# Moving a small partial result to another buffer and reordering VectorE's work in a fused cross-attention kernel

## The chip, the cores and the metric

The kernel runs on one core of a Trainium2 chip. The metric is the device time of one execution in microseconds (us). Engines are named as in the profile: PE is TensorE's matmul stream and PEld its weight loads, DVE is VectorE, ACT is ScalarE, POOL is GpSimd, SP is SyncE, which here only issues transfers. A queue named SPq or POOLq is the stream of transfers that this engine issues.

## The reference

For each of 8 batches, with x1 and x2 of shape 512 x 1024 (channels by positions), Wq and Wk of 64 x 512 and Wv of 512 x 512, all in fp32:

```python
q = jnp.einsum('bcn,dc->bnd', x1, Wq) + bq
k = jnp.einsum('bcn,dc->bdn', x2, Wk) + bk[:, None]
v = jnp.einsum('bcn,dc->bdn', x2, Wv) + bv[:, None]
attn = jax.nn.softmax(jnp.einsum('bnd,bdm->bnm', q, k), axis=2)
attn_out = jnp.einsum('bcm,bnm->bcn', v, attn)
return attn_out + x1
```

## The kernel before, in words

**What is multiplied.** The value projection and the attention product are taken in another order: first y = x2 times the exponentials of the scores (512 channels by 1024 query positions), then out = Wv times y, plus bias, plus x1. Both of these are done by Strassen's scheme (Winograd's form) over 2 x 2 blocks: seven block products instead of eight, at the price of sums of blocks on DVE, on transfers that add, and in PSUM. For y the seven products carry the numbers 1, 2, 6, 7, 5, 3, 4, and most of these are themselves done by the same scheme one level down. The function `multiply_seeded` does one such product: seven inner products named by steps 1, 7, 6, 2, 5, 4, 3 in this order. It needs left sums (`left_stream`, line 569, four DVE instructions) and right sums (`right_stream`, lines 599, 604 and 606, three DVE instructions) ahead of it.

**What one product does on ACT.** Inside `multiply_seeded`, PE accumulates steps 1, 6, 5 and 4 in one PSUM tile, the chain, and ACT copies the chain after each of them into the quarters of the product's two result banks b0 and b1 (line 858). Step 7 goes to a second PSUM tile, the third. ACT copies it to SBUF as a small tile v, also at line 858. Only after these copies can PE go on adding into the chain. At the end DVE adds v into bank b1; this is `complete`, line 875. In the profile the chain of product 5 is ps_i5chain, its third ps_i5third, its banks ps_ya, and the v of every product is just v.

**How work is ordered.** The order on each engine is the order in which the program is written; there is no scheduler. `period(s, n, nn, nnn)` is one batch: s is the batch whose y and output are made, n the next one, whose scores and exponentials are made at the same time, nn and nnn the ones after. Batches are counted from 0. `s.six` is true for batches 2 to 5, in which product 6 of y is also done by the inner scheme and products 6 and 7 are joined. For such a batch the stretch that matters runs on PE as follows: scores of batch n, queries of nn (ps_q, line 192), product 7, product 5, product 3, more scores of n (ps_s, line 237), and then the keys of nn (ps_k, line 192).

**Buffers and waits.** An SBUF tile is asked for with a tag. Two tiles with the same tag and one buffer share the same memory, so the first write to the later tile waits for everything that still reads or writes the earlier one, transfers too. Four tags count here:

- `r` holds, within one batch, v of product 5, v of product 3, v of product 4, and then the output block 12 of the batch (uo3 in the program). That block gets x1 added by a POOL transfer and is stored by an SP transfer (lines 1058 and 1059, `out_dram<-uo` in the profile), both issued in the next batch.
- `yT4` holds the left sums of product 7 and later the sum T4 of y.
- `a12` holds a block of x2, and then the left sums of product 3.
- `eT2` holds T2, a sum of exponential blocks that two POOL transfers read (line 386, `eT<-eT`), and then the right sums of product 3.

**The row sums.** `shares` inverts the softmax's row sums of one half: a DVE reciprocal (line 320), a POOL transfer to memory (line 321), and a POOL transfer that spreads them over the partitions (line 327, `den<-row`). `lower` subtracts the maximum from the next batch's scores (DVE, line 342). `copy_7` copies product 7's two banks to SBUF, negated (ACT, line 975); its second call reads bank b1, so it comes after product 7's `complete`. `join_67` adds that to product 6 (DVE, line 970).

**The lines that the change touches** are those between product 7 and product 5 of `period`. Product 7's matmuls are recorded earlier; `complete_7` is its joining on DVE.

Of the kernel before, what the change touches and what calls it, by code (L numbers as in the profile page):

```python
# [15 lines left out]
def kernel(  # L16
# [295 lines left out]
    def invert(s, h):  # L312

        few = s.few[h]
        s.row[h] = row = dram.tile([1, H], F32, tag="row", name=f"row_{s.b}_{h}")
        to = row.rearrange("o (p f) -> (o p) f", p=P)
        if h == 0 and s.b > 1:
            nc.vector.tensor_tensor(few[:, 0, :], few[:, 0, :], few[:, 1, :], ALU.add)
            to = row.rearrange("o (z p f) -> (o p) z f", z=2, p=D)
        nc.vector.reciprocal(few, few)  # L320
        nc.gpsimd.dma_start(to, few)

    def spread(s, h):

        s.rden[h] = s.den[h]
        queue = nc.sync if s.b >= B - 2 else nc.gpsimd
        queue.dma_start(s.rden[h], s.row[h].broadcast_to([P, H]))

    def shares(s, h):
        invert(s, h)  # L330
        spread(s, h)
# [7 lines left out]
    def lower(s, h, i):  # L339
        e = s.e[h][:, :, i, :]  # L340
        top = s.top[h].unsqueeze(1).to_broadcast([P, 2, H])
        nc.vector.tensor_tensor(e, e, top, ALU.subtract)  # L342
# [193 lines left out]
    def weave(*streams):  # L536

        streams = list(streams)
        while streams:
            for stream in list(streams):  # L540
                if next(stream, "end") == "end":
                    streams.remove(stream)
# [19 lines left out]
    def left_stream(s, i, x, tag):  # L562

        v = {f"{p + 1}{q + 1}": x[:, ts(q, MH // 2), ts(p, P)] for p in range(2) for q in range(2)}
        sums = sb.tile([P, 4, MH // 2, P], F32, tag=tag, name=f"aI{i}_{s.b}")
        s.inner[i] = v
        for z, (k, x, y, op) in enumerate(LEFT_SUM if i in (1, 2) else LEFT):
            v[k] = sums[:, z]
            nc.vector.tensor_tensor(v[k], v[x], v[y], op)  # L569
            yield  # L570
# [4 lines left out]
    def right_stream(s, i, x, *tags):  # L575

        half = x.shape[1] // 2
        v = {f"{q + 1}{r + 1}": x[:, ts(q, half), ts(r, H // 2)] for q in range(2) for r in range(2)}
        last = 4 // len(tags)
        shape = [P, last, half, H // 2]  # L580
        sums = [
            sb.tile(shape, F32, tag=t, name=f"eI{i}{t}_{s.b}") if isinstance(t, str) else t for t in tags
        ]
        if i in (1, 2):
            for z, k in enumerate(("T1", "T2", "T4", "T3")):
                v[k] = sums[z // last][:, z % last]
            s.inner[i, "t"], s.inner[i, "m"] = v, sums[-1][:, last - 2 : last]
            for k, x, y, op in (
                ("T3", "22", "12", ALU.add),
                ("T2", "T3", "11", ALU.subtract),  # L590
                ("T1", "12", "11", ALU.subtract),
                ("T4", "21", "T2", ALU.subtract),
            ):
                nc.vector.tensor_tensor(v[k], v[x], v[y], op)
                yield
            return
        both, t2, t4 = sums[0][:, 0:2], sums[-1][:, last - 2], sums[-1][:, last - 1]
        part = x.rearrange("p (q k) (r n) -> p q k r n", q=2, r=2)
        nc.vector.tensor_tensor(
            both, part[:, :, :, 1, :], part[:, 0].rearrange("p k r n -> p r k n"), ALU.subtract  # L600
        )
        s.inner[i, "t"] = v | {"T1": both[:, 0], "T3": both[:, 1], "T2": t2, "T4": t4}
        yield
        nc.vector.tensor_tensor(t2, both[:, 0], v["22"], ALU.subtract)
        yield
        nc.vector.tensor_tensor(t4, v["21"], t2, ALU.add)
        yield

    def inner_right(s, i, x, *tags):
        weave(right_stream(s, i, x, *tags))  # L610

    def inner_product(s, i, z, ps, opens, *copies):

        ka, kb, _, _ = MULT[z]
        n_k = s.inner[i][ka].shape[1]
        for k in range(n_k):
            nc.tensor.matmul(  # L617
                ps,
                s.inner[i][ka][:, k, :],
                s.inner[i, "t"][kb][:, k, :],  # L620
                start=opens and k == 0,
                stop=z in (2, 3, 4) and k == n_k - 1,
                skip_group_check=True,
            )
        for copy in copies:
            nc.scalar.copy(copy, ps)

    def inner_parts(s, i):

        ks = ("third", "chain") if i in ((1, 6, 7) if s.six else (2, 7)) else ("chain", "third")  # L630
        of = {k: ps_s.tile([P, H], F32, tag="s", name=f"ps_i{i}{k}_{s.b}")[:, left] for k in ks}
        return of["chain"], of["third"]
# [202 lines left out]
    def multiply_seeded(s, i, v_tag, hooks={}, bank=None):  # L835

        bank = bank or MULT[i][2]

        def fresh(j):
            s.bank[bank, j] = ps = ps_a.tile(  # L840
                [P, H], F32, tag=f"{bank}{j}", name=f"ps_y{bank}{j}_{s.b}_{i}"
            )
            return ps

        b0 = fresh(0)
        chain, third = inner_parts(s, i)
        if v_tag == "top" or s.b == B - 1 and v_tag == "r":
            v = sb.tile([P, H], F32, tag="top", name=f"v{i}_{s.b}", bufs=2)[:, left]
        else:
            v = sb.tile([P, 2, H], F32, tag=v_tag, name=f"v{i}_{s.b}")[:, 0, left]  # L850
        seeded = s.six and i == 5
        if seeded:
            nc.scalar.copy(third, s.v6)

        def step(z, ps, opens, out=None, of=None):
            inner_product(s, i, z, ps, opens)
            if out is not None:
                nc.scalar.copy(out, of)  # L858
            if z in hooks:
                hooks[z]()  # L860

        step(1, chain, True, b0[:, left], chain)
        step(7, third, not seeded, v, third)
        if s.six and i == 6:
            s.v6 = v
        b1 = fresh(1)
        step(6, chain, False, b1[:, left], chain)
        step(2, b0[:, left], False)
        step(5, chain, False, b0[:, right], chain)
        step(4, b1[:, left], False, b1[:, right], chain)  # L870
        step(3, b0[:, right], False)

        def complete(b1=b1):
            b = b1.rearrange("p (a n) -> p a n", a=2)
            nc.vector.tensor_tensor(b, b, v.unsqueeze(1).to_broadcast([P, 2, H // 2]), ALU.add)

        return complete
# [91 lines left out]
    def join_67(s):  # L969
        nc.vector.tensor_tensor(s.tmp[6], s.tmp[6], s.tmp[7], ALU.add)  # L970

    def copy_7(s, j):
        if j == 0:
            s.tmp[7] = sb.tile([P, 2, H], F32, tag="u1", name=f"uy7_{s.b}")
        nc.scalar.mul(s.tmp[7][:, j, :], s.bank["c", j], -1.0)
# [253 lines left out]
    def period(s, n, nn, nnn):  # L1229
# [72 lines left out]
        if s.b == 0:  # L1302
# [30 lines left out]
            complete_5 = multiply_seeded(s, 5, "r")  # L1333
# [21 lines left out]
        else:  # L1355
# [78 lines left out]
            else:  # L1434
                complete_5 = multiply_seeded(s, 5, "top", {6: evict_q} if five and nn else {}, "a")
# [8 lines left out]
                    leave()  # L1444
            if n:
                sums_3 = right_stream(s, 3, s.t["22"], "eT2" if s.six else "eT1")
                next(sums_3)
                if s.b == 1:
                    shares(s, 1)
                weave(*([left_stream(s, 3, s.a["S4"], "a12" if s.six else "aI3")] if nn else []), sums_3)  # L1450
                if s.six:
                    complete_7()
                    shares(s, 1)
                lower(n, 0, 0)
            else:
                inner_right(s, 3, s.t["22"], "eT1")
            hooks = {}
            if s.six:
                lower(n, 0, 1)
                complete_5 = multiply_seeded(s, 5, "r", {7: lambda: copy_7(s, 0), 6: lambda: copy_7(s, 1)}, "a")  # L1460
                join_67(s)
                complete_5()
                evict_y(s, "22")
            else:
                complete_7 = multiply_seeded(s, 7, "y12")
                complete_7()
                hooks[7] = lambda: copy_7(s, 1)
                copy_7(s, 0)
# [237 lines left out]
    with tc.manual_schedule():  # L1706
        head(states[0])
        for b in range(B):
            period(*states[b : b + 4])
# [36 lines left out]
```

## Time and profile before

| what | value |
|---|---|
| median of 3 runs | 671.51 us (671.10 to 671.86) |
| the profiled execution's own time | 671.32 us |
| span of the profile, first to last instruction | 669.5 us |
| PE busy | 658.5 us, 98% |
| DVE busy | 619.1 us, 92% |
| ACT, POOL busy | 387.0 us (58%), 215.8 us (32%) |
| moved by transfers | 133.26 MB, mean 199 GB/s |
| granted TensorE clock | 1.000 |

The 1.8 us between the span and the execution's own time lie before the first and after the last instruction. The share of busy PE says that PE is nearly always occupied, so a change can gain only where PE stands still, or by giving PE less to do. The mean busy share of the core's 16 transfer engines appears as "DMA share"; it can come out a little over 1 in a short window.

### The profile page before, as it was taken

Reading aid. Unit: us, or ns where it says so; the run is one execution under the profiler, and the core shown is the slowest. Engines: PE = TensorE matmul, PEld = TensorE weight load, DVE = VectorE, ACT = ScalarE, POOL = GpSimd, SP = SyncE. Lnnn points to the kernel's source line nnn. Section 1 sums busy time; section 2 is a strip of 40 time slices with the busy share of each in tenths; the row PEclk is TensorE's granted clock in tenths of the full one; section 3 lists DMA queues with packets and bytes.
Section 4 is the critical chain, followed back from the end, with each engine's and each line's share of the span. In section 5 each row is a group of like instructions: output and inputs, shape, how many; then the busy total and the mean of one; then the engine's idle time right before and its main releaser. Section 6 shows DMA issues by size and latency. Waiting matters only on the chain.

```text
span 669.5 us, 8115 instructions
## 1 busy us (share of the span) xinstructions
PE 658.5 (98%) x2644; PEld 436.7 (65%) x2644; DVE 619.1 (92%) x900; ACT 387.0 (58%) x744; POOL 215.8 (32%) x187
## 2 busy tenths in 40 slices
PE   9999999999999999998999999999999999999997
PEld 4435755766668666776667676676765757657865
DVE  1999999989999899998989989999889999999996
ACT  3754457446485666764667646766467455484332
POOL 0126214621328203282033710346103640224300
PEclk9999999999999999999999999999999999999999
DMA  8688578994899959999599995989956895368614
GB/s 334 248 250 269 129 245 150 211 266 133 261 174 211 262 156 285 187 190 271 141 283 187 192 286 152 260 197 185 284 145 126 186 239 173 67 131 181 126 39 150
DMA packets 48522, 133.26 MB, mean 199 GB/s; under 512 B 5600, under 2 KB 6112, under 8 KB 48480
## 3 DMA queue, kind: packets, MB, share of 16 engines
q0 software_dynamic: 21488, 59.32, 48.7%
q1 hardware_dynamic: 26848, 73.29, 30.2%
q8 instruction: 21, 0.34, 0.2%
q10 hardware_dynamic: 144, 0.14, 0.1%
q14 instruction: 21, 0.17, 0.1%
HBM read 87.83 MB, written 16.81 MB: 156 GB/s over the span
## 4 chain that ended last, share of the span: by engine, by line
PE 83%; DMA 8%; DVE 5%; ACT 2%; issue 1%; SPq 0%; ACTq 0%
PE ps_yc L617 8%; PE ps_ya L617 7%; PE ps_oc L504 7%; DMA out_dram<-uo 6%; PE ps_s L237 5%; PE ps_ya L504 4%; PE ps_oa L504 4%; PE ps_k L192 3%; PE ps_oa L801 3%; PE ps_i4b L952 3%; PE ps_i3chain L617 3%; PE ps_i1chain L617 3%; PE ps_i2chain L617 3%; PE ps_i5chain L617 3%; PE ps_q L192 3%; PE ps_oc L952 2%
## 5 line engine op out<-in xcount | busy, mean ns | idle before, releaser
L342 DVE TENSOR_TENSOR e<-e,top 128x1024 f32<-128x1024 f32 x60 | 72.0, 1216 | 0.2 <-POOL top L274 0.2
L351 ACT ACTIVATE e<-e 128x1024 f32<-128x1024 f32 x60 | 62.9, 1060 | 15.8 <-DVE e L342 15.5
L274 POOL PARTITION_ALL_REDUCE top<-max x16 | 32.3, 2019 | 110.6 <-DVE max L268 51.7
L246 ACT COPY e<-ps_s 128x512 f32<-128x512 f32 x90 | 47.8, 623 | 9.7 <-PE ps_s L237 7.1
L237 PE MATMUL ps_s<-q,k 64*128 64x512 f32 (+1 forms) x188 | 46.6, 598 | 0.0
L306 POOL PARTITION_ALL_REDUCE den<-sum x10 | 33.3, 3333 | 31.4 <-DVE sum L268 26.5
L258 DVE TENSOR_TENSOR max<-max,e 128x1024 f32<-128x1024 f32 x30 | 36.5, 1218 | 0.3
L237 PEld LDWEIGHTS ps_s<-q,k 64*128 64x128 f32 x188 | 17.5, 186 | 19.9 <-issue 16.5
L987 DVE TENSOR_TENSOR y<-y,den 128x1024 f32<-128x1024 f32 x24 | 29.2, 1219 | 0.3
L858 ACT COPY ps_yc<-ps_i7chain 128x256 f32<-128x256 f32 x32 | 11.4, 357 | 28.9 <-PE ps_i7chain L617 15.1
L287 POOL PARTITION_ALL_REDUCE den<-sum x6 | 19.4, 3230 | 21.9 <-DVE sum L268 21.9
L192 PE MATMUL ps_q<-x_in_x_dram,wqk_sb 128*64 128x512 f32 x112 | 25.6, 598 | 0.4
L504 PE MATMUL ps_oc<-yT,w 128*128 128x512 f32 x56 | 25.3, 594 | 0.1
L504 PE MATMUL ps_oa<-yT,w_S 128*128 128x512 f32 x56 | 25.2, 593 | 0.0
L569 DVE TENSOR_TENSOR aI<-a 128x256 f32<-128x256 f32 x60 | 24.7, 411 | 0.0
L617 PE MATMUL ps_yc<-e,aI 128*128 128x256 f32 x92 | 23.6, 379 | 0.0
L858 ACT COPY ps_ya<-ps_i5chain 128x256 f32<-128x256 f32 x32 | 11.7, 365 | 20.2 <-PE ps_i5chain L617 16.2
L258 DVE TENSOR_TENSOR max<-e 128x1024 f32<-128x1024 f32 x15 | 18.3, 1218 | 5.0 <-POOL den L306 3.1
L858 ACT COPY ps_ya<-ps_i1chain 128x256 f32<-128x256 f32 x28 | 10.0, 357 | 21.8 <-PE ps_i1chain L617 16.8
L170 POOL DMA_DIRECT2D aS<-in_x2T_dram x7 | 6.3, 897 | 49.1 <-ACT aS L166 49.1
L858 ACT COPY ps_yc<-ps_i3chain 128x256 f32<-128x256 f32 x32 | 11.4, 357 | 18.2 <-PE ps_i3chain L617 13.9
L192 PE MATMUL ps_k<-x_in_x_dram,wqk_sb 128*64 128x512 f32 x96 | 21.9, 598 | 0.0
(395 smaller groups left out, 1897.5 us busy)
## 6 DMA issues: line engine op xcount, KB each, us to landing
x_in_x_dram<-in_x_dram SPq DMA_DIRECT2D x60, 512.0 KB, 7.9
a<-in_x2T_dram SPq DMA_DIRECT2D x32, 512.0 KB, 7.9
eT<-eT POOLq DMA_DIRECT2D x24, 512.0 KB, 8.3
aS<-in_x2T_dram POOLq DMA_DIRECT2D x21, 512.0 KB, 5.8
uo<-in_x_dram POOLq DMA_DIRECT2D x17, 512.0 KB, 9.9
e<-e POOLq DMA_DIRECT2D x13, 512.0 KB, 7.5
r<-in_x_dram POOLq DMA_DIRECT2D x11, 512.0 KB, 6.9
out_dram<-r SPq DMA_DIRECT2D x11, 512.0 KB, 3.7
```

Source lines behind the costliest of these rows:

```text
L192: nc.tensor.matmul(ps[r, :], w_sb[:, c, :], s.x[:, c, ts(h, H)], start=(c == 0), stop=(c == CT - 1),)
L237: nc.tensor.matmul(ps[g][:, n], s.k[r, ts(i, P)], s.q[r, ts(h, H)][:, n], start=True, stop=True)
L246: nc.scalar.copy(e[:, g, i, :], ps[g])
L258: nc.vector.tensor_tensor(f, e[:, :, 0, :] if i == 1 else f, e[:, :, i, :], op)
L274: nc.gpsimd.partition_all_reduce(s.top[h], s.mx[h][:, 0, :], P, ReduceOp.max)
L306: nc.gpsimd.partition_all_reduce(s.den[h], s.mx[h][:, 0, :], P, ReduceOp.add)
L342: nc.vector.tensor_tensor(e, e, top, ALU.subtract)
L351: nc.scalar.activation(e, e, AF.Exp)
L504: nc.tensor.matmul(ps, left[ka][:, k, ts(j, P)], right[kb][:, k, :], start=opens and k == 0, stop=i in (2, 3, 4) and k == n_k - 1, skip_gr ...
L617: nc.tensor.matmul(ps, s.inner[i][ka][:, k, :], s.inner[i, "t"][kb][:, k, :], start=opens and k == 0, stop=z in (2, 3, 4) and k == n_k - 1 ...
L858: nc.scalar.copy(out, of)
L952: nc.tensor.matmul(ps, s.inner[i][ka][:, k, :], s.inner[i, "t"][kb][:, k, :], start=opens and k == 0, stop=z in (2, 3, 4) and k == n_k - 1 ...
```

## The change

Three edits, all inside `period`, and all for batches 2 to 5 alone (`s.six`). The other batches keep the order that they had.

1. The v of y's product 5 is taken from the tag `yT4` and no longer from `r`. The copy of its third (line 858) writes it.
2. On DVE, the four left sums of product 3 now stand together and first; before they were interleaved with the three right sums, which began.
3. On DVE, the reciprocal of `shares(s, 1)` and product 7's `complete_7` now stand between product 3's left sums and its right sums; before they stood behind both, with `complete_7` first. The POOL transfers that `shares` issues keep their place in POOL's order.

```diff
                     leave()
             if n:
                 sums_3 = right_stream(s, 3, s.t["22"], "eT2" if s.six else "eT1")
-                next(sums_3)
-                if s.b == 1:
+                if s.six:
+                    weave(left_stream(s, 3, s.a["S4"], "a12"))
                     shares(s, 1)
-                weave(*([left_stream(s, 3, s.a["S4"], "a12" if s.six else "aI3")] if nn else []), sums_3)
-                if s.six:
                     complete_7()
-                    shares(s, 1)
+                    weave(sums_3)
+                else:
+                    next(sums_3)
+                    if s.b == 1:
+                        shares(s, 1)
+                    weave(*([left_stream(s, 3, s.a["S4"], "aI3")] if nn else []), sums_3)
                 lower(n, 0, 0)
             else:
                 inner_right(s, 3, s.t["22"], "eT1")
             hooks = {}
             if s.six:
                 lower(n, 0, 1)
-                complete_5 = multiply_seeded(s, 5, "r", {7: lambda: copy_7(s, 0), 6: lambda: copy_7(s, 1)}, "a")
+                complete_5 = multiply_seeded(s, 5, "yT4", {7: lambda: copy_7(s, 0), 6: lambda: copy_7(s, 1)}, "a")
                 join_67(s)
                 complete_5()
                 evict_y(s, "22")
```

How the instructions move is shown for batch 3; batches 2, 4 and 5 are alike. First ACT, from the beginning of product 5 to product 3. Here v5 and v3 are the small tiles of the two products, ps_ya0 and ps_ya1 the banks of product 5, uy7 the copy of product 7, and behind "waits" stand the engines or transfer counters that the instruction waits for: DMAHW is a transfer issued by SP, DMASW one issued by POOL.

```order
 L853 COPY ps_i5third_3_2115<-v6_3_1971 128x256 [waits Activation_49]
 L858 COPY ps_ya0_3_5_2113<-ps_i5chain_3_2114 128x256 [waits PE_49,Activation_49]
-L858 COPY v5_3_2116<-ps_i5third_3_2115 128x256 [waits DMAHW4_49,DMASW0_49,PE_49]
+L858 COPY v5_3_2116<-ps_i5third_3_2115 128x256 [waits DMASW5_49,DVE_49,PE_49]
 L975 ACTIVATE uy7_3_2124<-ps_yc0_3_7_2069 128x512 [waits DMAHW2_49,DMASW7_49]
 L858 COPY ps_ya1_3_5_2126<-ps_i5chain_3_2114 128x256 [waits PE_49,Activation_49]
@@ -332,10 +332,10 @@
 L858 COPY ps_ya1_3_5_2126<-ps_i5chain_3_2114 128x256 [waits PE_49]
 L858 COPY ps_yc0_3_3_2146<-ps_i3chain_3_2147 128x256 [waits PE_49,Activation_49]
-L858 COPY v3_3_2149<-ps_i3third_3_2148 128x256 [waits DVE_49,PE_49]
+L858 COPY v3_3_2149<-ps_i3third_3_2148 128x256 [waits DMAHW4_49,DMASW0_49,PE_49]
```

No instruction of ACT changes its place. The wait for the store of block 12 (DMAHW4) and for the transfer that added x1 to it (DMASW0) passes from v5 to v3, the next tile in `r`. In its place v5 waits for the earlier holders of `yT4`: a POOL transfer of the batch before (DMASW5), the DVE instructions that wrote product 7's left sums, and PE.

Second, DVE between the last maximum of the next batch's scores and `lower`. eI3 and aI3 are product 3's right and left sums, few is the reciprocal's tile, ps_yc1 is bank b1 of product 7. Before:

```order
L599 TENSOR_TENSOR eI3eT2_3_2097<-e_3_1_1634 128x1024
L569 TENSOR_TENSOR aI3_3_2099<-aS4_3_1902 128x256
L604 TENSOR_TENSOR eI3eT2_3_2097<-eI3eT2_3_2097,e_3_1_1634 128x512
L569 TENSOR_TENSOR aI3_3_2099<-aI3_3_2099,aS4_3_1902 128x256
L606 TENSOR_TENSOR eI3eT2_3_2097<-e_3_1_1634,eI3eT2_3_2097 128x512
L569 TENSOR_TENSOR aI3_3_2099<-aS4_3_1902 128x256
L569 TENSOR_TENSOR aI3_3_2099<-aS4_3_1902,aI3_3_2099 128x256
L875 TENSOR_TENSOR ps_yc1_3_7_2079<-ps_yc1_3_7_2079,v7_3_2072 128x512
L320 RECIPROCAL few_3_1_1958<-few_3_1_1958 128x4
```

And now, the same place on DVE:

```order
L569 TENSOR_TENSOR aI3_3_2097<-aS4_3_1902 128x256
L569 TENSOR_TENSOR aI3_3_2097<-aI3_3_2097,aS4_3_1902 128x256
L569 TENSOR_TENSOR aI3_3_2097<-aS4_3_1902 128x256
L569 TENSOR_TENSOR aI3_3_2097<-aS4_3_1902,aI3_3_2097 128x256
L320 RECIPROCAL few_3_1_1958<-few_3_1_1958 128x4
L875 TENSOR_TENSOR ps_yc1_3_7_2079<-ps_yc1_3_7_2079,v7_3_2072 128x512
L599 TENSOR_TENSOR eI3eT2_3_2107<-e_3_1_1634 128x1024
L604 TENSOR_TENSOR eI3eT2_3_2107<-eI3eT2_3_2107,e_3_1_1634 128x512
L606 TENSOR_TENSOR eI3eT2_3_2107<-e_3_1_1634,eI3eT2_3_2107 128x512
```

The same nine instructions stand there. The three right sums, of which the first waits for the transfers that read `eT2`, moved behind product 7's joining.

## The prediction

> **What bounds the kernel now.** I read the page first: shares of engines, then the chain that ended last.
>
> ```profile
> span 669.5 us, 8115 instructions
> PE 658.5 (98%) x2644; PEld 436.7 (65%) x2644; DVE 619.1 (92%) x900; ACT 387.0 (58%) x744; POOL 215.8 (32%) x187
> PE 83%; DMA 8%; DVE 5%; ACT 2%; issue 1%; SPq 0%; ACTq 0%
> ```
>
> PE stands still for 669.5 - 658.5 = 11.0 us in all, so no reordering can bring more than that. The chain gives 8% to transfers, and these are the place to look. The table of waits between 160 and 500 us (batches 2 to 5; columns: total, times, longest) names one, and PE waits that come as often:
>
> ```profile
> ACT v L858 <- DMA out_dram<-uo: 7.4, 3, 2.7
> PEld ps_i5chain L617 <- ACT ps_ya L858: 5.8, 3, 2.1
> PE ps_i5chain L617 <- ACT ps_ya L858: 4.5, 3, 1.7
> ```
>
> Three times ACT cannot write v5, since the store of the last batch's output block, the earlier holder of tag r, has not landed. The chain in order of time shows how that reaches PE in batch 3, and that batches 4 and 5 have the same store in it (start, length, what):
>
> ```profile
> 299.87 0.93 PE ps_q L192 x3
> ...
> 301.00 12.66 DMA out_dram<-uo
> ...
> 313.76 0.04 ACT v L858
> ...
> 314.02 0.60 ACT uy L975
> 314.63 0.29 ACT ps_ya L858
> ...
> 314.96 1.13 PE ps_i5chain L617 x4
> ...
> 383.12 12.18 DMA out_dram<-uo
> ...
> 465.03 12.16 DMA out_dram<-uo
> ```
>
> The store lands at 313.66, v5 is copied, behind it on ACT come copy_7 and the chain's copy into ps_ya, and PE's next step of product 5 waits for that last copy. Batch 2 has no such stall, though its program is the same, so it is the measure. The windows from the first query matmul to the next ps_s matmul of batches 2, 3, 4 and 5:
>
> ```profile
> core 0: us, PE busy (x) PEld busy (x) DVE busy (x) ACT busy (x) POOL busy (x), PEclk, DMA share, GB/s
> 219.58:241.75 22.17, 22.17 (x102) 16.87 (x102) 20.08 (x31) 11.91 (x27) 4.20 (x5) 1.00 1.01 274
> 299.87:323.86 23.99, 22.25 (x102) 16.90 (x102) 21.29 (x33) 11.82 (x27) 4.34 (x6) 1.00 1.03 274
> 381.98:405.50 23.52, 22.25 (x102) 16.90 (x102) 20.83 (x33) 11.82 (x27) 4.34 (x6) 1.00 1.02 269
> 463.62:487.39 23.77, 22.24 (x102) 16.90 (x102) 21.11 (x33) 11.82 (x27) 4.01 (x6) 1.00 1.01 263
> ```
>
> Same 102 matmuls, same clock of 1.00, and 1.82, 1.35 and 1.60 us more than batch 2: 4.77 us.
>
> **The change part by part. First, v5 in yT4.** This takes the store out of v5's wait. In its place come product 7's left sums, which PE has read before it reaches product 5's third, so that the wait for PE covers them, and the transfer of the batch before into y's T4, long landed:
>
> ```profile
> 261.75 0.92 POOL L1572 DMA_DIRECT2D yT<-y  x1 [2.58 <-DVE y L987]
> yT<-y POOLq DMA_DIRECT2D x5, 512.0 KB, 4.7
> ```
>
> 261.75 + 4.7 = 266.5, against v5 at about 311.5. Cost 0. So batches 3 to 5 should come down to batch 2's length: **-4.77 us**.
>
> **Second, the wait goes to v3.** ACT in batch 2:
>
> ```profile
> 231.24 0.37 ACT L858 COPY v<-ps_i5third 128x256 f32<-128x256 f32 x1 [0.45 <-PE ps_i5third L617]
> 233.42 0.60 ACT L975 ACTIVATE uy<-ps_yc 128x512 f32<-128x512 f32 x1 [0.91 <-DVE ps_yc L875]
> 233.92 0.38 ACT L858 COPY ps_ya<-ps_i5chain 128x256 f32<-128x256 f32 x1
> 237.55 0.37 ACT L858 COPY v<-ps_i3third 128x256 f32<-128x256 f32 x1 [0.43 <-DVE ps_ya L875]
> ```
>
> Counted from the first query matmul (219.58 here), v5 is wanted at +11.66 and v3 at +17.54 (237.55 less the 0.43 for which it waits on product 5's joining, since that reads v5 in the same tile; this wait goes too). The store lands at +13.79, +13.32 and +13.57 in batches 3 to 5 (301.00 + 12.66 - 299.87, and so on). Too late for v5 by about 2, early enough for v3 by 3.7 to 4.2 us. Bounds: below, nothing; above, a store as slow as the slowest SP transfer issued there, 16.9 us (row further down), which would land at +18.0 and cost 0.5 in each of three batches, 1.5 us. I take nothing: the three landings differ by half a microsecond.
>
> **Third, DVE's order.** Nothing is added; what moves is what waits behind what. Before, in batch 3:
>
> ```profile
> 306.54 0.68 DVE L268 TENSOR_TENSOR max<-max 128x512 f32<-128x512 f32 x1
> 309.92 1.23 DVE L599 TENSOR_TENSOR eI3eT<-e 128x1024 f32<-128x1024 f32 x1 [2.70 <-DMA eT<-eT]
> 311.06 0.42 DVE L569 TENSOR_TENSOR aI<-aS 128x256 f32<-128x256 f32 x1
> ...
> 313.61 0.69 DVE L875 TENSOR_TENSOR ps_yc<-ps_yc,v 128x512 f32<-128x512 f32 x1
> 314.21 0.17 DVE L320 RECIPROCAL few<-few 128x4 f32<-128x4 f32 x1
> 314.30 2.33 DVE L342 TENSOR_TENSOR e<-e,top 128x1024 f32<-128x1024 f32 x2
> 308.94 0.36 ACT L858 COPY ps_yc<-ps_i7chain 128x256 f32<-128x256 f32 x1 [0.51 <-PE ps_yc L617]
> ```
>
> DVE idles 2.70 us before the first right sum while four left sums of 0.42, the reciprocal and L875 (0.69) stand behind it. Now the left sums fill 307.2 to 308.9 and the reciprocal 0.17 more; L875 waits for ACT's last copy of product 7 (308.94 + 0.36 = 309.3) and ends at 310.0; the right sums (1.23 + 0.68 + 0.68) end near 312.5. Product 3's step 7 on PE, the first that needs both, would stand at 316.7 without the stall (its four matmuls lie right ahead of the row at 237.25 below: 237.25 - 0.86 = 236.4 in batch 2, plus 299.87 - 219.58). So neither sum is on the path, and `lower` starts at 312.5, not 314.30, as much earlier as PE gets. What this buys is L875, 4.3 us earlier. In batch 2 it held copy_7 for 0.91 on ACT (233.42), thereby the chain's copy (233.92), and PE shows a small stretch right behind it:
>
> ```profile
> 237.25 1.05 PE ps_i3chain L617 x4
> ...
> 319.54 0.86 PE ps_i3chain L617 x4
> ```
>
> 1.05 - 0.86 = 0.19 in batch 2, which the stalled batch 3 does not show. With edit 1 alone all four batches would look so; with L875 early it should go: up to 4 x 0.19 = 0.76 us, at worst 0. Between them I take 0.5: the link from ACT to PE is read from one batch.
>
> **Fourth, POOL.** The write of the inverted sums and their spreading (256 KB) come some 5 us earlier (the reciprocal at 309.1, not 314.2) into a stretch whose transfers are saturated (share 1.01 to 1.03). At 274 GB/s they cost 0.96 us of it. Who needs the transfers next are the keys, whose x is on its way:
>
> ```profile
> 304.01 5.32 SPq L139 DMA_DIRECT2D x_in_x_dram<-in_x_dram  x4
> x_in_x_dram<-in_x_dram SPq DMA_DIRECT2D x2, 512.0 KB, 15.6
> x_in_x_dram<-in_x_dram SPq DMA_DIRECT2D x2, 512.0 KB, 16.9
> 327.42 3.65 PE L192 MATMUL ps_k<-x_in_x_dram,wqk_sb 128*64 128x512 f32 x16
> ```
>
> The middle rows are the landings of the last pair in batches 3 and 5. The fourth load, issued at about 308.0, lands at 323.6; keys would start at 325.6 instead of 327.4 and read the fourth tile 2.7 us later, at 328.3. Margin 4.7; in batch 5, by the same working (472.0 + 16.9 = 488.9 against 492.1), 3.2. Both exceed 0.96, so nothing is charged.
>
> **Sum.** 4.77 + 0.5 = 5.3 us. The profiled execution took 671.32 (its span and 1.8 around it), 0.19 under the median of the runs; less 5.3 it is 666.0, and from the median **666.2 us**. Behind the stretch all runs in PE's tow: the chain of batch 6 goes through DVE for 37 us, but it enters at a copy of a PE result and moves with it:
>
> ```profile
> 558.31 0.36 ACT ps_yc L858
> ...
> 594.61 0.61 DVE ps_oc L831
> ```
>
> **The rivals.** B: the wait comes back smaller, at v3, by the 1.5 us bounded above. Gain 3.8, time 667.7. For it: SP's queue is full there. Against: it needs a landing 4 us later than any of three.
>
> C: no change, 671.5. Either v5's wait was not the last one, or the stretch is bound by its transfers and hands the time to another. For it: a share above 1. Against: batch 2 moved its transfers at the same share 1.01 in 22.17 us. A rule that points to C is in the Trainium skill, page "DMA: Bandwidth & Descriptors", section on the anatomy of one DMA: a transfer takes about 2.0 us plus its bytes over 436 GB/s. By my estimate from that page, 512 KB would land in 3.2 us, at 304.2, long before v5 asks, and freeing v5 from it would give nothing. The trace does not agree: 12.66, 12.18 and 12.16 us for the same size.
>
> D: slower. The mechanism is v3 again, with a store that lands much later than now because the order of POOL's transfers around it shifts. ACT stands at v3, behind it the chain's copies of product 3, behind them PE, one us for one us. It decides from +17.54 + 5.3/3 = +19.3; at +20.5, a landing of 19.4 us, each batch loses 3.0: 666.2 + 9.0 = 675.2. For it: v3 now really has this wait. Against: no store or load in these batches took over 16.9 us.
>
> **How the numbers follow.** Forecast 0.78, B 0.08, C 0.08, D 0.06. A measurement of this kernel can tell about 0.2%, 1.3 us, from no change. Forecast and B are faster by more: 0.86; C is the same: 0.08; D slower: 0.06. The forecast's own range is 665.5 to 667.0 (gain between 4.5 and 6.0: 4.77 or 5.53, and the runs' spread of 0.4). The range reaches into B: 665.3 to 668.5.
>
> **What would show it.** Right: the wait of ACT's v for `out_dram<-uo` is gone and the windows above take 22.0 to 22.2 us in all four batches; v3 in batches 3 to 5 has no wait for a transfer; L875 of product 7 ends before copy_7 is due, so that the wait of 0.91 is gone; the 1.05 is 0.86. Wrong in a step: v waits for `out_dram<-uo` at product 3 (B or D); windows near 22.4 (the 0.19 stays); windows as long as before with another name in front of PE (C); keys that wait for x.

## The result, and the profile after

| | before | changed |
|---|---|---|
| median | 671.68 us (671.10 to 673.03, 4 runs) | **666.11 us** (665.95 to 666.30, 4 runs) |
| ratio | | **0.9914**, 95% interval 0.9897 to 0.9931 |
| the profiled execution | 671.32 us, span 669.5 | 665.95 us, span 664.2 |

The changed kernel is 0.86% faster, and its 95% interval does not include 1. By the medians it gains 5.57 us, by the two profiled executions 5.37.

The head of the changed kernel's page, and the first line of its chain:

```profile
span 664.2 us, 8111 instructions
PE 658.2 (99%) x2644; PEld 437.4 (66%) x2644; DVE 622.9 (94%) x900; ACT 387.2 (58%) x744; POOL 215.5 (32%) x187
PE 84%; DVE 10%; ACT 2%; DMA 1%; issue 1%; POOL 1%; SPq 0%; DVEq 0%
```

PE stands still for 664.2 - 658.2 = 6.0 us instead of 11.0. In the chain transfers fell from 8% to 1%, and what is left are loads at the very start; no store stands in it any more. DVE's busy time rose by 3.8 us although its 900 instructions are the same; the last section accounts for 2.9 of it.

The four stretches from the first query matmul to the next ps_s matmul, batches 2 to 5, in the windows of the changed kernel:

```profile
core 0: us, PE busy (x) PEld busy (x) DVE busy (x) ACT busy (x) POOL busy (x), PEclk, DMA share, GB/s
219.59:241.76 22.17, 22.17 (x102) 16.91 (x102) 22.07 (x33) 11.91 (x27) 4.30 (x5) 1.00 1.03 278
299.88:321.86 21.98, 21.98 (x102) 16.98 (x102) 21.86 (x33) 11.90 (x27) 4.44 (x6) 1.00 1.05 275
379.97:401.95 21.98, 21.98 (x102) 16.98 (x102) 21.88 (x33) 11.90 (x27) 4.45 (x6) 1.00 1.05 272
460.07:482.05 21.98, 21.98 (x102) 16.98 (x102) 21.56 (x32) 11.90 (x27) 4.46 (x6) 1.00 1.05 273
```

In each row the length and PE's busy time are now the same number: PE never stands still there. Batch 2 kept its 22.17; batches 3 to 5 fell from 23.99, 23.52 and 23.77 to 21.98, which is 2.01 + 1.54 + 1.79 = **5.34 us**, the whole gain of the span. They fell 0.19 below batch 2, by which the prediction had measured them. Part of what they lost was counted as busy: before, PE was busy for 22.25, 0.27 more than now. That is the first group of product 5's chain behind the stall, which took 1.13 (314.96 in the chain of before) where such a group takes 0.86.

The table of waits between 160 and 500 us of the changed kernel has no line any more in which ACT's v waits for `out_dram<-uo`. The lines of v5 and v3, and one that names another transfer:

```profile
ACT v L858 <- PE ps_i5third L617: 1.8, 4, 0.5
...
ACT v L858 <- PE ps_i3third L617: 1.1, 3, 0.5
...
ACT v L858 <- DMA row<-few: 0.5, 1, 0.5
```

The last line is v3 in batch 4. There the profile puts the wait down to the small write of the inverted sums, with which v3 has nothing to do in the program. It is as long as v3's wait for PE in batches 3 and 5 (0.45), so it costs nothing.

ACT in batch 3, which had stood still until 313.76. The rows are v5, the second copy_7 (it reads what product 7's L875 writes) and v3, and below them that L875 on DVE:

```profile
311.53 0.37 ACT L858 COPY v<-ps_i5third 128x256 f32<-128x256 f32 x1 [0.45 <-PE ps_i5third L617]
...
312.72 0.60 ACT L975 ACTIVATE uy<-ps_yc 128x512 f32<-128x512 f32 x1
...
317.58 0.37 ACT L858 COPY v<-ps_i3third 128x256 f32<-128x256 f32 x1 [0.45 <-PE ps_i3third L617]
```

```profile
309.43 0.67 DVE L875 TENSOR_TENSOR ps_yc<-ps_yc,v 128x512 f32<-128x512 f32 x1
```

L875 ends at 310.10, copy_7 has no wait, and v3, which has inherited the wait for the store, waits here for its product's third alone.

### The profile page after: what moved, and what is told of

It reads as the page before. It is cut to its first block, busy times and chain, and to the rows that moved or that the text cites. A ratio compares the mean times of both kernels' runs of the same rounds, so it can differ in the third digit from the quotient of the medians.

```text
span 664.2 us, 8111 instructions
## 1 busy us (share of the span) xinstructions
PE 658.2 (99%) x2644; PEld 437.4 (66%) x2644; DVE 622.9 (94%) x900; ACT 387.2 (58%) x744; POOL 215.5 (32%) x187
## 4 chain that ended last, share of the span: by engine, by line
PE 84%; DVE 10%; ACT 2%; DMA 1%; issue 1%; POOL 1%; SPq 0%; DVEq 0%
PE ps_yc L617 9%; PE ps_ya L617 7%; PE ps_oc L504 7%; PE ps_s L237 4%; PE ps_oa L504 4%; PE ps_q L192 3%; PE ps_i5chain L617 3%; PE ps_i7chain L617 3%; PE ps_k L192 3%; PE ps_ya L504 3%; PE ps_oa L801 3%; PE ps_i4b L952 3%; PE ps_i3chain L617 3%; PE ps_i1chain L617 3%; PE ps_i2chain L617 3%; PE ps_oc L952 2%
## 5 line engine op out<-in xcount | busy, mean ns | idle before, releaser
L569 DVE TENSOR_TENSOR aI<-a 128x256 f32<-128x256 f32 x60 | 26.8, 447 | 0.0
L327 POOL DMA_DIRECT2D den<-row x12 | 6.7, 560 | 57.8 <-DMA row<-few 42.7
L504 PE MATMUL ps_oc<-yT,w 128*128 128x512 f32 x56 | 25.3, 594 | 0.2 <-DVE uo L1051 0.2
L858 ACT COPY ps_ya<-ps_i5chain 128x256 f32<-128x256 f32 x32 | 11.5, 361 | 21.6 <-PE ps_i5chain L617 17.3
```

The lines of the kernel that those rows point to most:

```text
L504: nc.tensor.matmul(ps, left[ka][:, k, ts(j, P)], right[kb][:, k, :], start=opens and k == 0, stop=i in (2, 3, 4) and k == n_k - 1, skip_gr ...
```

## The experiments

**Two theories.** The first is the prediction's: v5's wait for the store is the cause, and DVE's order adds a little. The rival is that the order does the work (product 7's joining was late on DVE, and ACT and PE behind it), with the tag as an accessory. The first two runs take one half of the change each; the others ask how much of DVE's order is needed, whether v3's wait costs something, and where batch 2's 0.19 and two odd durations come from.

### tag_only: the tag alone

The kernel before with v5 in yT4; DVE's order stays as it was.

```diff
-                complete_5 = multiply_seeded(s, 5, "r", {7: lambda: copy_7(s, 0), 6: lambda: copy_7(s, 1)}, "a")
+                complete_5 = multiply_seeded(s, 5, "yT4", {7: lambda: copy_7(s, 0), 6: lambda: copy_7(s, 1)}, "a")
```

> The tag alone: v of product 5 in yT4, DVE's order as in the kernel before. Theory 'the order is needed too': product 7's joining (L875) still stands behind product 3's right sums, which wait for the transfer that reads eT2 until about +10.0 us after the first query matmul; it ends at about +14.4, the second copy of product 7 at about +15.0, the chain's copy at about +15.4 instead of +14.6, so PE stalls about 0.8 us in each of batches 3 to 5: windows of 22.8 us instead of 21.98, time about 668.7 us. Rival 'the tag is all': windows of 22.0 to 22.2, time 666.1 to 666.5.

Measured: 668.20 us (667.68 to 669.09), ratio 0.9946 (0.9928 to 0.9963): 3.5 of the 5.6 us. That is near what the theory "the order is needed too" had expected, 668.7, and outside the range of its rival. The windows of its batches 2 and 3:

```profile
219.37:242.26 22.89, 22.44 (x102) 16.83 (x102) 20.04 (x31) 11.83 (x27) 4.21 (x5) 1.00 1.01 269
300.37:322.94 22.57, 22.25 (x102) 16.90 (x102) 19.86 (x31) 11.83 (x27) 4.36 (x6) 1.00 1.05 273
```

Batches 4 and 5 take 22.56 each. The store's wait is gone, and PE still stands still for 22.57 - 22.25 = 0.32 us in batch 3, nearly as long in 4 and 5 and 0.45 in batch 2, and pays the 0.27 behind it. Its waits name the new last one:

```profile
DVE eI3eT L599 <- DMA eT<-eT: 10.9, 4, 2.8
...
ACT uy L975 <- DVE ps_yc L875: 6.2, 4, 1.7
```

DVE stands for up to 2.8 us at the right sums, whose buffer two POOL transfers still read. Behind them stands L875 of product 7, and behind that, on ACT, copy_7 and the chain's copy. This wait had been there all along; in batches 3 to 5 the store's came out later and hid it. That batch 2 shows it here, and hardly did before, is a matter of when those transfers landed. The first right sum of batch 2 in the kernel before, and then with the tag alone:

```profile
229.01 1.23 DVE L599 TENSOR_TENSOR eI3eT<-e 128x1024 f32<-128x1024 f32 x1 [2.09 <-DMA eT<-eT]
```

```profile
229.56 1.23 DVE L599 TENSOR_TENSOR eI3eT<-e 128x1024 f32<-128x1024 f32 x1 [2.85 <-DMA eT<-eT]
...
233.97 0.60 ACT L975 ACTIVATE uy<-ps_yc 128x512 f32<-128x512 f32 x1 [1.67 <-DVE ps_yc L875]
```

The right sum waits 0.76 us longer, and so does copy_7: 1.67 instead of 0.91. In the kernel before, batch 2 had neither the store's wait nor a long one here. Why the transfers landed earlier there is not shown by one trace of each kernel.

### order_only: DVE's order alone

The changed kernel with v5 back in r.

```diff
-                complete_5 = multiply_seeded(s, 5, "yT4", {7: lambda: copy_7(s, 0), 6: lambda: copy_7(s, 1)}, "a")
+                complete_5 = multiply_seeded(s, 5, "r", {7: lambda: copy_7(s, 0), 6: lambda: copy_7(s, 1)}, "a")
```

> DVE's new order alone, v of product 5 stays in r. Both theories: v still waits for the store of the last batch's block, the stall of 1.5 to 2.0 us in batches 3 to 5 stays, time 671.3 us give or take 0.5. Were the order worth something by itself, the windows of batches 3 to 5 would fall below 23.5 and the time below 670.5.

Measured: 672.24 us (669.95 to 674.54), ratio 1.0001 (0.9984 to 1.0019). No gain that can be measured, though the interval has room for about 1 us either way; the median lies 0.4 above the range that had been expected. The profiled execution, 670.24 us, is one of the shorter. Its windows are 22.28, 22.53, 23.59 and 23.95 us: batch 3 alone is clearly shorter than before, since the store landed earlier there and v5 waited 1.22 for it and not 2.68. Its waits keep the store:

```profile
ACT v L858 <- DMA out_dram<-uo: 6.1, 3, 2.6
...
PE ps_i5chain L617 <- ACT ps_ya L858: 3.3, 3, 1.7
```

So the rival falls: the order without the tag is worth nothing that these runs can tell. But the tag without the order is not the whole gain either. By the medians the halves bring 3.5 and nothing, and both together 5.6: the order's 2.1 us can be had only when the store is out of the way, as always with two waits of which the later one counts.

### left_first: how much of the order is needed

The changed kernel, in which only the left sums stand ahead; the reciprocal and product 7's joining are back behind the right sums.

```diff
                 if s.six:
                     weave(left_stream(s, 3, s.a["S4"], "a12"))
-                    shares(s, 1)
-                    complete_7()
                     weave(sums_3)
+                    complete_7()
+                    shares(s, 1)
```

> The tag, and product 3's left sums ahead of its right sums, but product 7's joining and the reciprocal behind both, as before. Theory 'what counts is when the joining is done, not its place': left sums end at about 309.4, right sums near 312.5, the joining at 313.1 (+13.2), product 7's second copy at +13.8, in time for the chain's copy at +14.2: windows 22.0, time 666.1 to 666.5. Rival 'the joining must stand ahead of the right sums': a stall as in the run with the tag alone, 667.5 to 668.7.

Measured: 666.59 us (665.70 to 666.97), ratio 0.9918 (0.9900 to 0.9935). By the medians 0.5 us are missing, which lies within the spread of the runs; the median lies 0.1 above the range of the theory and 0.9 below that of its rival. The trace shows more. The windows of its batches 3 and 5 (batches 2 and 4 are 22.16 and 21.99):

```profile
300.43:322.41 21.98, 21.98 (x102) 16.98 (x102) 21.10 (x31) 11.99 (x27) 4.35 (x6) 1.00 1.06 277
...
460.62:483.06 22.44, 22.25 (x102) 16.90 (x102) 20.86 (x31) 11.82 (x27) 3.94 (x5) 1.00 1.04 274
```

One batch stalls and one does not, in one execution. The row of the second copy_7 on ACT in the two batches tells why:

```profile
314.07 0.60 ACT L975 ACTIVATE uy<-ps_yc 128x512 f32<-128x512 f32 x1 [0.71 <-DVE ps_yc L875]
...
474.96 0.60 ACT L975 ACTIVATE uy<-ps_yc 128x512 f32<-128x512 f32 x1 [1.41 <-DVE ps_yc L875]
```

A wait of 0.71 costs nothing; one of 1.41 makes PE stand still for 22.44 - 22.25 = 0.19. Hence ACT has some 1.41 - 0.19 = 1.2 us in hand there. The kernel with the tag alone agrees: its copy_7 waits 1.54 in batch 3, 0.32 of it reach PE, and 1.54 - 0.32 = 1.2; in batch 2 it is 1.67 - 0.45 = 1.2. Past that, PE pays one for one, and the 0.27 of the restart on top. What counts is thus that the joining is done in time, not that it stands ahead of the right sums: with the four left sums ahead, DVE uses the time in which it would wait for the transfers, and the joining comes out early enough in three batches of four.

### after_swap and before_swap: the order of the two stores

Each batch has two output blocks left that are stored in the next one. In batches 2 to 5 the block in r goes first. Here it goes second, so that it lands later: once in the changed kernel, where v3 waits for it, once in the kernel before, where v5 does.

```diff
-            n.leave = [last, leave] if n.six else [last] if five else [leave, last]
+            n.leave = [leave, last] if n.six else [last] if five else [leave, last]
```

> The changed kernel, with the two deferred stores of batches 2 to 5 in the other order: block 22 first, block 12 (the tile that v of product 3 waits for) second. The second store landed at 303.5 + 11.5 = 315.0 in batch 3 before, +15.1 after the first query matmul, and v of product 3 is wanted at +17.5 to +17.7. Theory 'v3 has room': no change, 666.1 us give or take 0.4. Rival 'v3 now bears the wait': longer than the changed kernel by the amount that the store is late, 1 us or more in each of four batches, 670.

> The kernel before, with the two deferred stores of batches 2 to 5 in the other order: block 22 first, block 12 (which holds r) second, so that it lands about 1.3 us later after the first query matmul in batches 3 to 5 (+15.1 instead of +13.8) and about 2.5 us later in batch 2 (+13.8 instead of +11.4). Theory 'v of product 5 waits for this very store': each later microsecond is paid: 3 x 1.3 and 2.1 in batch 2, some 6 us more, 677.5 us; windows of 24.3, 25.3, 24.9, 25.1. Rival 'the store is named by the profile but another thing ends the wait': no change, 671.5.

Measured: in the changed kernel 665.99 us (665.79 to 666.50), ratio 0.9914 (0.9897 to 0.9930), no difference to the changed kernel's own 666.11. The store of block 12 landed at 303.43 + 11.2 = 314.6 us in batch 3, 1.0 later than without this edit (301.00 + 12.6). The row of v3 there:

```profile
317.40 0.37 ACT L858 COPY v<-ps_i3third 128x256 f32<-128x256 f32 x1 [0.45 <-PE ps_i3third L617]
```

v3 asks at 317.40 - 0.45 = 316.95 and does not wait for it. In the kernel before the same edit gives 681.22 us (680.13 to 683.30), ratio 1.0147 (1.0123 to 1.0172), 9.7 us slower, where 6 had been expected. The waits of the latter:

```profile
PEld ps_i5chain L617 <- ACT ps_ya L858: 13.1, 4, 3.6
...
PE ps_i5chain L617 <- ACT ps_ya L858: 11.5, 4, 3.2
...
ACT v L858 <- DMA out_dram<-uo: 11.2, 3, 3.8
```

ACT's wait grew from 7.4 to 11.2 in batches 3 to 5, batch 2 has one now as well (4.1, for the store of r), and PE's grew from 4.5 to 11.5. The same edit that costs 9.7 us where v5 waits for the store costs nothing where v3 does. That settles the cause, and that v3 has time in hand, still 2.3 us with the later store in batch 3. PE's waits grew by 11.5 - 4.5 = 7.0 in the profiled execution, which took 683.30, 12.0 more than that of the kernel before; most of the rest is the clock, in the last section, which the expectation did not have. The windows that it gave, 24.3, 25.3, 24.9 and 25.1, came out at 27.28, 26.74, 26.62 and 25.11: right in batch 5, where the clock stayed at 1.00, and 1.4 to 3.0 us too low in the others.

### act_shift: batch 2's 0.19

The prediction put the 0.19 in batch 2 down to copy_7's wait of 0.91. That wait is gone, and the 0.19 is not: the row of 1.05 stands in batch 2 of the changed kernel too, and the copy ahead of it on ACT is product 3's own:

```profile
237.26 1.05 PE ps_i3chain L617 x4
```

```profile
236.76 0.36 ACT L858 COPY ps_yc<-ps_i3chain 128x256 f32<-128x256 f32 x1 [1.70 <-PE ps_i3chain L617]
```

The table of waits between 160 and 500 us names this pair once, in the kernel before as in the changed one:

```profile
PEld ps_i3chain L617 <- ACT ps_yc L858: 0.3, 1, 0.3
```

That copy should follow its matmuls as its likes do in the other batches, where it waits 1.42 for them. The matmuls end when they always do, the copy starts 0.27 late, and the profile shows nothing else for which it waits. If that hangs on where the instruction stands in ACT's program, it should move or go when some instructions are put in far ahead. This kernel has six copies of one column more at the very start:

```diff
                 nc.scalar.activation(warm[:, 0:1], warm[:, 0:1], AF.Exp)
+        for _ in range(6):
+            nc.scalar.copy(warm[:, 1:2], warm[:, 0:1])
```

> The changed kernel with six one-column copies added on ACT in its idle start, at about 8 us, so that each later instruction stands six places further in ACT's program. In batch 2 of every kernel so far the first copy of product 3's chain starts 0.27 us late and PE loses 0.19 us, whatever the order on DVE. Theory 'it hangs on the place in ACT's program': it leaves this copy and batch 2's window falls to 21.98 (or the loss shows up six instructions earlier). Rival 'it hangs on the data or on the other engines in batch 2': it stays, window 22.17. Time 666.1 give or take 0.4 either way.

Measured: 666.04 us (665.83 to 667.41), ratio 0.9919 (0.9899 to 0.9940). In its trace the copy in batch 2 waits 1.43, as elsewhere, the line of waits above is gone, and batch 2's window is as short as the others:

```profile
236.75 0.36 ACT L858 COPY ps_yc<-ps_i3chain 128x256 f32<-128x256 f32 x1 [1.43 <-PE ps_i3chain L617]
```

```profile
219.85:241.83 21.98, 21.98 (x102) 16.98 (x102) 21.66 (x32) 11.90 (x27) 4.30 (x5) 1.00 1.04 277
```

So the 0.19 has nothing to do with copy_7, with DVE's order or with the tag. It goes when ACT's program is six instructions longer ahead of it. What in the place of an instruction delays it by 0.27 us is not shown. The six copies' own cost and the 0.19 lie below what the medians can tell.

### left_early: two odd durations on DVE

In the changed kernel's trace one left sum of product 3 takes 1.15 us where its likes take 0.42, in all four batches. The row right behind the first left sum, batch 2, DVE:

```profile
226.84 0.42 DVE L569 TENSOR_TENSOR aI<-aS 128x256 f32<-128x256 f32 x1
227.30 1.15 DVE L569 TENSOR_TENSOR aI<-aI,aS 128x256 f32<-128x256 f32 x1
228.37 0.41 DVE L569 TENSOR_TENSOR aI<-aS 128x256 f32<-128x256 f32 x1
```

POOL starts its reduction over the partitions 0.27 us before:

```profile
227.03 1.88 POOL L274 PARTITION_ALL_REDUCE top<-max  x1 [3.90 <-DVE max L268]
```

Either the two engines get in each other's way, or the second left sum is slow since it reads what the first has just written. Here the left sums stand ahead of the last maximum, for which the reduction waits, so that they cannot meet:

```diff
                 weave(folds(n, 0, "max", ALU.max), *sums)
+                weave(left_stream(s, 3, s.a["S4"], "a12"))
                 highest(n, 0)
...
                 if s.six:
-                    weave(left_stream(s, 3, s.a["S4"], "a12"))
                     shares(s, 1)
```

> The changed kernel, with product 3's four left sums moved ahead of the last maximum's folding, so ahead of POOL's all-reduce; nothing else. In the changed kernel the second left sum takes 1.15 us instead of 0.42, in all four batches. Theory 'it is blocked by the all-reduce that runs beside it on POOL': the four take 0.42 each now, the all-reduce runs about 1.3 us later and whichever two-input instruction on DVE runs beside it, the reciprocal's follower or the first right sum, is the long one; time 666.1 give or take 0.4. Rival 'it is long since it reads the sum right before it': the second left sum stays at 1.15.

Measured: 666.35 us (666.06 to 666.70), ratio 0.9922 (0.9900 to 0.9944), the changed kernel's time within the error. The second left sum, and the right sum that now stands beside the reduction:

```profile
226.77 0.43 DVE L569 TENSOR_TENSOR aI<-aI,aS 128x256 f32<-128x256 f32 x1
...
229.12 0.70 DVE L875 TENSOR_TENSOR ps_yc<-ps_yc,v 128x512 f32<-128x512 f32 x1 [0.57 <-ACT ps_yc L858]
229.73 1.22 DVE L599 TENSOR_TENSOR eI3eT<-e 128x1024 f32<-128x1024 f32 x1
```

```profile
228.57 1.78 POOL L274 PARTITION_ALL_REDUCE top<-max  x1 [5.36 <-DVE few L320]
```

The left sum has its usual length though it still follows the one that it reads: the second reading falls. The reduction is shorter too, 1.78 instead of 1.88. What had been expected besides, a long first right sum, did not come: it starts 1.16 us into the reduction and takes its usual 1.22, and L875, which starts 0.55 us in, takes 0.70.

## Why the prediction was right, and where not

The forecast was 666.2 us and the time 666.11, within its own range of 665.5 to 667.0. The total came out nearly exactly; two of its parts did not.

- **v5's wait for the store (4.77 us): right in its cause, too small in its size.** The wait is gone, PE's stalls with it, and undoing this part alone takes the whole gain away. What failed is the sentence "So batches 3 to 5 should come down to batch 2's length". They came down to 21.98, and the term measured 5.34. Batch 2 was taken as the undisturbed length and had a delay of its own, 0.19, which the other three did not share. The better measure stood in the same rows: PE's busy time contains the 0.27 of a slow first group behind each stall, and 22.25 - 0.27 = 21.98.
- **"With edit 1 alone all four batches would look so": wrong.** With the tag alone they take 22.56 to 22.89, and the kernel 668.2. The order is not worth a small 0.5 on top of the tag: of the gain by the medians it carries 668.20 - 666.11 = 2.1 us. The row for this was quoted (L599's wait of 2.70 for a transfer) and so was L875 behind it at 313.61. What was not asked is what that time would cost once the store had gone. v5 would be copied at 311.5 and the second copy_7 be due 1.27 later, as in batch 2 (233.42 - 0.91 - 231.24), at 312.8; L875 ends at 313.61 + 0.69 = 314.3. That makes a wait of 1.5, which is what the tag's run showed (1.54 in batch 3), against the 1.2 that ACT has in hand. Instead, batch 2's wait of 0.91 was taken for all four.
- **DVE's new order: right.** L875 runs at 309.43 in batch 3 and ends at 310.10; predicted was 310.0. The right sums end at 312.8, near the predicted 312.5. One left sum took 0.73 longer than its likes, but that delayed L875 by only 0.1, since until 309.3 it would have waited for ACT's copy. None of it is on the path.
- **The 0.5 for L875's earlier place, read from the row of 1.05: wrong.** Its signs are of both kinds: copy_7's wait of 0.91 went, as predicted, and the 1.05 stayed. A wait of 0.91 lies below the 1.2 that ACT has in hand, and could not have reached PE. The 1.05 belongs to product 3's chain, and the table of waits of the kernel before already named product 3's own copy ahead of it; copy_7 delays a copy of product 5. The 0.19 stands in batch 2 alone, and it went when that copy stood six instructions later in ACT's program. The prediction noted that the link was read from one batch and took 0.5 of the possible 0.76; that this comes so near to 3 x 0.19 = 0.57 is luck, not reasoning. 4.77 + 0.5 and 5.34 + 0 agree because the 0.19 was misplaced twice: it was counted in three batches as still to be lost, and then as won.
- **v3 at no cost: right.** v3 has no wait for the store, and with a later store the time stays the same. The sign "v3 in batches 3 to 5 has no wait for a transfer" is not met to the letter: in batch 4 one is named, at no cost. Rivals B and D fall: the landing they needed did not come. (For B's range of 665.3 to 668.5 the prediction gives no working.) The same edit on the kernel before shows the size of what they feared, 9.7 us.
- **POOL's earlier transfers at no cost: right.** The keys run through in 3.58 us, without a wait for a transfer, and the stretch moves its bytes at a share of 1.03 to 1.05. The spreading of the sums came not 5 us but only 0.9 to 1.5 us earlier in batches 2 and 3 (239.30 for 240.19, 319.79 for 321.31), though its write is issued 4.3 to 4.9 earlier: that small write took the longer to land, and POOL waited for it.
- **Rival C, no change: wrong here, with a grain of truth.** It said that v5's wait might not have been the last one. In the tag's half alone another wait came right behind it, and took back 2.1 us. The sum that C takes from the Trainium skill, page "DMA: Bandwidth & Descriptors", section "Anatomy of one DMA — SWDGE (gpsimd) path", is fitted there on transfers issued by GpSimd. The store is issued by SP, so its 12.66 us shows that the sum does not serve for this store, and not that the section is wrong.

## What to carry to other kernels

When a stall goes, ask at once what would have been late next on the same engine, and look for it among the waits that the stall hid: two waits that end within a microsecond or two of each other are one problem, and either cure alone looks weak or worthless. Take the clean length of a stretch from its work (its instructions at their usual durations) rather than from the best example, which may have a fault of its own. And before an instruction's lateness is charged to the bottleneck, work out the time in hand between them; here 1.2 us, which a later run with two doses in one execution showed directly.

## What the runs showed of the hardware that was not expected

**A stall of some 3 us can be paid twice, the second time in clock.** In the kernel before with the stores swapped, the windows of batch 2 around PE's stall of 3.16 us (the columns are those of the windows above; the granted clock is the third number from the end):

```profile
231.00:233.00 2.00, 1.62 (x8) 1.09 (x6) 2.00 (x6) 0.00 (x0) 0.00 (x0) 1.00 1.04 355
233.00:235.00 2.00, 0.00 (x0) 0.00 (x0) 2.00 (x5) 0.42 (x2) 0.38 (x1) 1.00 1.06 379
235.00:237.00 2.00, 1.22 (x4) 1.00 (x5) 2.00 (x3) 1.25 (x3) 0.19 (x1) 0.77 0.97 318
237.00:239.00 2.00, 2.00 (x6) 1.64 (x5) 0.70 (x1) 0.36 (x1) 0.00 (x0) 0.50 1.05 343
239.00:241.00 2.00, 2.00 (x9) 1.69 (x9) 1.26 (x3) 0.36 (x1) 0.00 (x0) 0.88 1.00 232
```

The clock falls to 0.50 as PE resumes and is back some 4 us later. In the slowest window PE does 6 matmuls where the next one, at 0.88, has 9. The stalls of 3.16, 2.80 and 2.69 in batches 2 to 4 were followed by it, and these batches took 26.6 to 27.3 us; the one of 2.86 in batch 5 was not, and it took 25.11 at a clock of 1.00. PE was busy for 24.12, 23.94 and 23.93 us in the first three and for 22.25 in batch 5, some 5 us more in all: with the 7.0 of waits about the 12.0 that this execution lost. Its mean clock is 0.992. The Trainium skill, page "TensorE: Matmul & The Clock Gate", sections "What's actually happening" and "HAM oscillation — how this bites in real kernels", says that the clock halves after a window of about 3.4 us without work, and that the window runs freely; the section "Why this matters for your kernels" puts the bound at about 3 us. The 0.50 agrees, and so does that a stall of a given length may or may not be hit; that stalls of 2.69 and 2.80 were hit, shorter than either figure, it does not lead one to expect. The kernel before seems to stand at the edge of this, though its traced execution, at a clock of 1.000, has no stall over 1.74 (23.99 - 22.25): of 28 executions, the seven with a mean clock of 0.997 took 673.3 to 674.8 us, the others, at 0.999 or 1.000, 669.2 to 673.0. No execution of a kernel with v5 in yT4 fell below 0.999, and those of one such kernel lie within 1.6 us of each other. So the change also made the time steadier; that it did so by keeping the stalls short is argued, not shown, since these executions have no trace.

**A vector instruction with two operands in SBUF can be held by a reduction on POOL.** The left sum with 1.15 instead of 0.42 us and the reduction with 1.88 instead of 1.78 are that. The Trainium skill, page "SBUF — State Buffer", section "Who interferes with whom", states the rule: a DVE instruction with two inputs in SBUF contends with a GpSimd instruction that reads SBUF, through a shared read port; one with a single such input does not, certain faster modes aside. The traces agree: left sums of two SBUF operands are held beside the reduction and free without it, while L875, with one operand in PSUM, runs at 0.70 beside it. The hold was 0.73 us, for a start 0.27 us into the reduction, and the runs show it for this start alone: left sums that start 1.34 us in, and a right sum that starts 1.16 us in, take their usual time while the reduction still runs. Four times 0.73 are the 2.9 us of DVE's busy time named at the start. All of it lay in DVE's spare time here and cost nothing.

**An instruction's place in its engine's program can cost 0.27 us.** The same copy, with the same waits, started 0.27 us late in batch 2 in every kernel whose ACT program was as long as the original's, and on time with six instructions more ahead of it. One thing moves with ACT's program: a transfer that carries instructions (queue q14 of the profile) starts between 240 and 241 us in the changed kernel, some 4 us behind the late copy, and between 235 and 236 us with the six copies. That it has to do with the delay is not shown; the mechanism stays open.
